# Node pass of a relational graph layer: gathered rows in a pool of their own, two blocks' sums by VectorE, 352 of 2048 weight columns by ScalarE and GpSimd

## The chip, the cores and the metric

One core of a Trainium2 chip runs the whole program in one launch. The time is device microseconds of that core. The engines have queues of their own: PE (TensorE, matmuls and transposes; PEld is its weight load), DVE (VectorE), ACT (ScalarE), POOL (GpSimd) and SP (SyncE, which issues most DMAs). Each works through its instructions in order and waits at semaphores for the others.

## The reference, cut to what matters

A graph layer with relations, a mixture of experts, a second graph network and a ternary feed-forward stage follow each other, each added to x (10000 rows of 512, float32). Only the first is touched:

```python
w = jnp.einsum('rb,bio->rio', att, basis)      # 2 relations, 30 bases of 512 x 512
x_j = x[col]                                   # 5000 edges
for r in range(NUM_RELATIONS):
    gate = jax.nn.sigmoid(x_j @ gate_w[r, :, 0])
    msgs.append(gate[:, None] * x_j @ w[r])
msg = jnp.where((edge_type == 0)[:, None], msgs[0], msgs[1])
agg = jax.ops.segment_sum(msg, row, num_segments=x.shape[0])
return agg + x @ root + bias
...
h = relu(rgcn_gate_layer(x, ..., basis1, att1, gate_w1, root1, bias1))
out = rgcn_gate_layer(h, ..., basis2, att2, gate_w2, root2, bias2)
```

x is layer-normalised before it enters.

## The kernel before

**The node pass** (`rgcn_nodes1`, L775 to L799) goes over 20 blocks of four tiles of 128 rows (the last has two tiles and 16 rows). For each it loads x (tile `x_in`, by `rows_to`, L141), normalises it into `xn` (statistics on DVE, L172 to L178, the scaling on ACT, L183), stores `xn` to `xn_d`, transposes it (PE L198, copies on ACT L202), multiplies by root (PE L790), copies PSUM into `o_nodes` on ACT (L794), adds the bias to the whole block on POOL (L796) and stores to `r1_d`. Loads and stores stand in SP's queue.

**Beside it**, in the same stretch, two sorts of the edges run (`sort_edges`, L224 to L377): one by source with 42 tiles, one by target with 40. Each has a loop of 40 rounds in which PE, ACT and DVE find the place of 128 edges (DVE L353, L358, L362) and POOL scatters their records (L363). Behind the loop POOL loads the sorted table back (L372, tile `srt`). **Also beside it** are the relations' weights (`relation_weights`, L655 to L673): for each of 30 bases a 1 MB load (L663) and on DVE two instructions over 128x2048 (L670), one a relation. Both layers' weights are summed here, but for the last six bases of the second layer, which come in the first edge pass. A scheduler orders all this on every engine, by estimated costs.

**The edge pass** (`rgcn_edges`, L675 to L773) has an order written out by hand for PE, ACT and DVE. For each of 42 tiles it gathers 128 rows (L644, tile `x`, FETCHED = 6 tiles ahead), multiplies them with the gates on DVE (L708), makes the matrix `same` (L719, L721), sums rows of equal target (L728), multiplies by the relation's weights (`put`, L750), copies (L755) and scatter-adds into DRAM (L649). `beside_1` puts other work into the rounds: the six bases, copies of x to `a2_d` (L846) and the placing of nodes. The pass runs twice, on `xn_d` into `r1_d` and, with a relu, on `r1_d` into `a2_d`.

**The next stage** loads root2, bias2 and small weights (L151, L146, L944 on), and then block by block `r_in` from `r1_d` and `x_in` from `a2_d` (L141); ACT takes the relu of `r_in` (L975), PE transposes it and multiplies by root2 (L987).

**Memory.** On-chip memory comes from pools that open and close like a stack. A tile in memory that an earlier pool held waits until that pool's last users are done. `x` and `gate` of the edge pass lie in pools opened after those of the node pass close.

Of the kernel before, what the change touches and what calls it, by code (L numbers as in the profile page):

```python
# [8 lines left out]
F32 = mybir.dt.float32  # L9
# [3 lines left out]
AF = mybir.ActivationFunctionType  # L13
OP = mybir.AluOpType
# [3 lines left out]
P = 128  # L18
N = 10000
D = 512  # L20
KC = D // P
# [14 lines left out]
NB = (N + 511) // 512  # L36
PARTS = 8
PER = NT // PARTS + 1
RELATIONS = 2
# [31 lines left out]
def gnn_ffn_kernel(ctx: ExitStack, tc: tile.TileContext, I, out, dram):  # L71
# [60 lines left out]
            nc.sync.dma_start(d[r0 : r0 + P, :], zero)  # L132


    def rows_to(sb, d, b, store=False):

        for n, a0, a1 in block_parts(b):
            r0 = (b * 4 + a0) * P
            v = d[r0 : r0 + n * (a1 - a0), :].rearrange("(a p) d -> p a d", p=n)
            s = sb[:n, a0:a1, :]  # L140
            nc.sync.dma_start(v, s) if store else nc.sync.dma_start(s, v)  # L141

    def row_broadcast(pool, d, width, name):
# [48 lines left out]
    def transposed(tp, pt, src, tiles, cols, name="xT", on_act=False):  # L192

        xT = tp.tile([P, KC, 512], F32, name=name)
        for k in range(KC):
            ps = pt.tile([P, 512], F32, name="ps_t")
            for a, n in tiles:
                nc.tensor.transpose(  # L198
                    ps[:, a * P : a * P + n], src[:n, a, k * P : (k + 1) * P], ident[:n, :n]
                )  # L200
            if on_act:
                nc.scalar.copy(xT[:, k, :cols], ps[:, :cols])  # L202
            else:
                copy_out(xT[:, k, :cols], ps[:, :cols])
        return xT
# [448 lines left out]

    def relation_weights(basis, att_d, pool, stream, tag):  # L655

        att = row_broadcast(pool, att_d, RELATIONS * BASES, f"att_{tag}")
        ws = pool.tile([P, RELATIONS, KC * D], F32, name=f"w_{tag}")

        def sums():  # L660
            for b in range(BASES):
                t = stream.tile([P, KC, D], F32, name="basis")
                nc.sync.dma_start(t, basis[b].rearrange("(k p) o -> p k o", p=P))  # L663
                tf = t.rearrange("p k o -> p (k o)")
                for r in range(RELATIONS):
                    c = att[:, r * BASES + b : r * BASES + b + 1]
                    if b == 0:
                        nc.vector.tensor_scalar(ws[:, r], tf, c, None, op0=OP.mult)
                    else:
                        nc.vector.scalar_tensor_tensor(ws[:, r], tf, c, ws[:, r], op0=OP.mult, op1=OP.add)  # L670
                yield

        return ws, sums()  # L673

    def rgcn_edges(tag, meta, src_d, relu, ws, gate_d, dst_d, beside):  # L675

# [3 lines left out]
        with ExitStack() as s:  # L680
# [2 lines left out]
            pk = s.enter_context(tc.tile_pool(name=f"re_pk_{tag}", bufs=1, space=PSUM))  # L683
            pa = s.enter_context(tc.tile_pool(name=f"re_pa_{tag}", bufs=2, space=PSUM))
            po = s.enter_context(tc.tile_pool(name=f"re_po_{tag}", bufs=2, space=PSUM))
            gate = row_broadcast(fix, gate_d, RELATIONS * D, "gate")
            of_rel = fix.tile([P, RT, RELATIONS], F32, name="of_rel")
            nc.vector.tensor_scalar(of_rel[:, :, 0], meta["attr"], 0.0, None, op0=OP.is_equal)
            nc.vector.tensor_scalar(of_rel[:, :, 1], meta["attr"], 0.0, None, op0=OP.not_equal)
# [5 lines left out]
            carry_on = {-1: acc}  # L695

            def fetch(t):
                got[t] = wk.tile([P, D], F32, name="x", bufs=FETCHED + 2)
                return gather(got[t], src_d, meta["gidx"][:, t : t + 1])

            def make_ready(t):
# [73 lines left out]
    def rgcn_nodes1(root, bias, pools):  # L775

        ld, tp, small, pt, po = pools
        for b in range(NB):
            tiles, parts, cols = block_tiles(b), block_parts(b), block_cols(b)
            x = ld.tile([P, 4, D], F32, name="x_in")  # L780
            rows_to(x, I["x"], b)
            xn = ld.tile([P, 4, D], F32, name="xn")
            layernorm(small, xn, x, tiles, parts, on_act=True)
            rows_to(xn, xn_d, b, store=True)
            xT = transposed(tp, pt, xn, tiles, cols, on_act=True)
            o = tp.tile([P, 4, D], F32, name="o_nodes")
            for a, n in tiles:
                ps_o = po.tile([P, D], F32, name="ps_o")
                for k in range(KC):
                    nc.tensor.matmul(  # L790
                        ps_o[:n], lhsT=xT[:, k, a * P : a * P + n], rhs=root[:, k, :],
                        start=k == 0, stop=k == KC - 1,
                    )
                nc.scalar.copy(o[:n, a, :], ps_o[:n])  # L794
            for n, a0, a1 in parts:
                nc.gpsimd.tensor_tensor(  # L796
                    o[:n, a0:a1], o[:n, a0:a1], bias[:n, None, :].to_broadcast([n, a1 - a0, D]), OP.add
                )
            rows_to(o, r1_d, b, store=True)  # L799

    with ExitStack() as s:
        wpool = s.enter_context(tc.tile_pool(name="w_rel", bufs=1))
        stream = s.enter_context(tc.tile_pool(name="stream", bufs=3))
        src_meta = s.enter_context(tc.tile_pool(name="src_meta", bufs=1))
        wk = s.enter_context(tc.tile_pool(name="sort", bufs=1))
        place_wk = s.enter_context(tc.tile_pool(name="place_wk", bufs=1))
        ps = s.enter_context(tc.tile_pool(name="sort_ps", bufs=2, space=PSUM))
        with ExitStack() as n:
            ld = n.enter_context(tc.tile_pool(name="ld1", bufs=2))
            tp = n.enter_context(tc.tile_pool(name="tp1", bufs=2))  # L810
            fix = n.enter_context(tc.tile_pool(name="fix1", bufs=1))
            small = n.enter_context(tc.tile_pool(name="small1", bufs=3))
            pt = n.enter_context(tc.tile_pool(name="pt1", bufs=2, space=PSUM))
            po = n.enter_context(tc.tile_pool(name="po1", bufs=3, space=PSUM))
            zero = fix.tile([P, D], F32, name="zero")
            nc.gpsimd.memset(zero, 0.0)
            for d in (r1_d, a2_d, xf_d, x2_d):
                clear_spare(zero, d)
            root = load_square(fix, I["L0_gnn_root1"], "root")
            bias = row_broadcast(fix, I["L0_gnn_bias1"], D, "bias")  # L820
            by_src = sort_edges(
                "s", I["src"], I["dst"], I["edge_type_2"], by_src_d, wk, ps, src_meta, by_relation=True
            )
            by_src = add_targets(by_src, wk, ps, src_meta)
            by_dst = sort_edges(
                "d", I["dst"], I["src"], I["edge_weight1"].rearrange("e o -> (e o)"), by_dst_d, wk, ps,
                meta_pool,
            )
            rgcn_nodes1(root, bias, (ld, tp, small, pt, po))
            ws1, adding = relation_weights(I["L0_gnn_basis1"], I["L0_gnn_att1"], wpool, stream, "1")  # L830
            for _ in adding:
                pass
            ws2, adding = relation_weights(I["L0_gnn_basis2"], I["L0_gnn_att2"], wpool, stream, "2")
            for _ in range(EARLY_BASES):
                next(adding)
        placing = place_nodes(by_dst, place_wk, ps, meta_pool)

        def beside_1(i, ready):
            if i > FETCHED and i % 6 == 2:
                next(adding, None)  # L840
            elif i > FETCHED and i % 2:
                next(placing, None)
            if i < ET:

                c0, c1 = N * i // ET, N * (i + 1) // ET
                cp = nc.sync.dma_start(a2_d[c0:c1, :], I["x"][c0:c1, :])  # L846
                tc.add_manual_dep(
                    cp.ins, ready.ins.name,
                    mybir.DependencyInfo(mybir.DependencyClass.Sync, mybir.DependencyReason.DATA),
                    reason="not all at once, and not beside the nodes",  # L850
                )

        rgcn_edges("1", by_src, xn_d, False, ws1, I["L0_gnn_gate_w1"], r1_d, beside_1)
        for _ in adding:
            pass
        rgcn_edges(
            "2", by_src, r1_d, True, ws2, I["L0_gnn_gate_w2"], a2_d, lambda i, _: next(placing, None)
        )
        for _ in placing:
            pass  # L860
# [1082 lines left out]
```

## Time and profile before

| | us |
|---|---|
| median of 3 runs (4553.06, 4539.74, 4551.91) | 4551.91 |
| profiled execution, and its span | 4526.65, 4524.6 |
| mean granted TensorE clock in it | 0.945 |
| node pass, sorts and weights | 0 to 517 on PE, to 534 on DVE |
| first edge pass | 547 to 785 |
| second edge pass | 786 to 1007 |
| later stages | from 1013 |

The page lists busy time by engine, slices of the span, the chain that ended last, and groups of instructions by line. In a group's row stand the busy time, the mean of one in ns, and after the second bar the idle time of its engine just ahead of it, with what ended it. A line such as `DVE L708 ... [9.58 <-DMA x]` in a timeline says that the engine sat idle for 9.58 us before it until a DMA into x had landed. Two more rows are used in what follows: POOL's other direct DMAs are few (L372 took 2.00 us to issue at 503.2 us), and SP's issues of stores to `r1_d` took 0.50 to 0.70 us each (525.0, 526.2 and 529.6 us). The large loads on SP are the bases (60 of 1 MB each), `x_in` and `r_in` (19 of 1 MB each).

### The profile page before, as it was taken

How to read it: one execution, taken by the hardware profiler on the slowest of the kernel's cores; microseconds unless marked ns; L12 is line 12 of the kernel's file. 1: busy time of each engine (PE TensorE's matmuls, PEld its weight loads, DVE VectorE, ACT ScalarE, POOL GpSimd, SP SyncE). 2: the span in 40 equal slices, each digit the busy share in tenths (PEclk: the TensorE clock that was granted, in tenths of full speed). 3: DMA queues.
4: the chain of work that ended last, by engine and by line, in shares of the span. 5: the costliest groups of instructions: out<-in, count | busy, mean ns of one | idle time of the engine just before them, and what ended most of it. 6: DMA issues, size and time to landing. Idle time of an engine off the chain costs nothing.

```text
span 4524.6 us, 43237 instructions
## 1 busy us (share of the span) xinstructions
PE 4026.9 (89%) x13663; PEld 2048.2 (45%) x13663; DVE 2825.3 (62%) x6089; ACT 1731.2 (38%) x3093; POOL 1558.0 (34%) x1128
## 2 busy tenths in 40 slices
PE   6889698999999927968789999999999999999997
PEld 3443354554444413434444545445554454544443
DVE  9988676755544565647565557545575455755776
ACT  4334222333333311126447223372232722335775
POOL 3424454540000066865551124211242112422443
PEclk9999899998989958989899999999999999999998
DMA  8766685557555316986421233012320123302332
GB/s 283 247 228 207 226 224 126 106 95 241 169 175 178 127 45 124 163 180 214 135 67 49 77 113 85 22 40 77 117 82 21 40 77 115 84 21 58 109 111 96
DMA packets 286241, 560.41 MB, mean 124 GB/s; under 512 B 41776, under 2 KB 72529, under 8 KB 284351
## 3 DMA queue, kind: packets, MB, share of 16 engines
q1 hardware_dynamic: 212304, 367.82, 24.1%
q0 software_dynamic: 73712, 189.84, 18.1%
q8 instruction: 111, 1.82, 0.2%
q14 instruction: 114, 0.93, 0.1%
HBM read 316.03 MB, written 262.00 MB: 128 GB/s over the span
## 4 chain that ended last, share of the span: by engine, by line
PE 38%; DVE 9%; DMA 3%; ACT 2%; issue 2%; POOL 1%; DVEq 0%; POOLq 0%; ACTq 0%
PE ps_b L1409 15%; PE ps_d L1409 9%; PE ps_o L1715 5%; PE ps_e L1409 4%; PE ps_x L1551 2%; PE ps_x L1337 2%; DMA x<-xg_d,gpos 2%; DVE stats L1524 2%; DMA x_in<-x_d,node_at 1%; DVE feat L1341 1%; PE ps_q L1783 1%; DVE feat L1424 1%; ACT feat L1537 1%; DVE x L1326 1%; DVE t L1455 1%
## 5 line engine op out<-in xcount | busy, mean ns | idle before, releaser
L1409 PE MATMUL ps_b<-feat,w 128*128 128x512 f32 (+1 forms) x1120 | 497.6, 586 | 6.9 <-ACT feat L1537 6.9
L1409 PE MATMUL ps_d<-feat,w_s 128*128 128x512 f32 (+1 forms) x1096 | 489.0, 583 | 3.6 <-ACT p L1417 2.7
L1417 ACT ACTIVATE feat<-ps_b,cols 128x512 f32<-128x512 f32 (+1 forms) x300 | 203.9, 681 | 535.3 <-PE ps_b L1409 522.6
L1463 POOL TENSOR_TENSOR feat<-feat 128x1024 f32<-128x1024 f32 (+1 forms) x70 | 162.7, 2324 | 626.5 <-DVE feat L1462 576.6
L790 PE MATMUL ps_o<-root,xT 128*128 128x512 f32 (+1 forms) x632 | 324.8, 630 | 0.0
L1478 POOL TENSOR_TENSOR feat<-feat,p 128x1024 f32<-128x1024 f32 (+1 forms) x66 | 167.2, 2533 | 455.4 <-ACT feat L1417 455.3
L1409 PEld LDWEIGHTS ps_b<-feat,w 128*128 128x128 f32 x1120 | 209.6, 192 | 239.2 <-issue 208.7
L750 PE MATMUL ps_o<-w,aT 128*128 x672 | 311.0, 607 | 1.1 <-issue 0.9
L670 DVE SCALAR_TENSOR_TENSOR w<-basis,att,w 128x2048 f32<-128x2048 f32 x116 | 307.0, 2657 | 0.0
L1553 DVE TENSOR_TENSOR x_rows<-ps_x,be 128x512 f32<-128x512 f32 (+1 forms) x237 | 157.6, 686 | 234.6 <-PE ps_x L1551 229.4
L1409 PE MATMUL ps_b<-t,w_s 128*128 128x512 f32 (+1 forms) x560 | 257.3, 600 | 33.5 <-ACT feat L1417 33.5
L1409 PEld LDWEIGHTS ps_d<-feat,w_s 128*128 128x128 f32 x1096 | 198.4, 191 | 195.2 <-issue 171.5
L987 PE MATMUL ps_n<-root,rT 128*128 128x512 f32 (+1 forms) x632 | 285.1, 607 | 0.0
L644 POOL DMA_INDIRECT x<-xg_d,gpos x160 | 177.6, 1110 | 259.4 <-PE ps_x L1337 49.6
L1409 PE MATMUL ps_e<-feat,w 128*128 128x512 f32 (+1 forms) x560 | 255.4, 595 | 9.2 <-DVE feat L1372 9.2
L1409 PE MATMUL ps_b<-feat,w_s 128*128 128x512 f32 (+1 forms) x560 | 250.0, 586 | 0.0
L1537 ACT ACTIVATE feat<-feat,bn_sm 128x512 f32<-128x512 f32 (+2 forms) x320 | 237.6, 805 | 3.6 <-DVE bn_sm L1515 3.6
L1524 DVE BATCH_NORM_STATS2 stats<-feat 128x6 f32<-128x512 f32 (+1 forms) x320 | 203.7, 668 | 41.5 <-POOL feat L1478 28.3
L1337 PEld LDWEIGHTS ps_x<-same,x 128*128 128x128 f32 x1280 | 164.3, 196 | 104.9 <-ACT x L1332 55.2
L1337 PE MATMUL ps_x<-same,x 128*128 128x128 f32 x1280 | 171.4, 283 | 42.9 <-ACT x L1332 36.8
L172 DVE BATCH_NORM_STATS2 ln_st<-x_in 128x6 f32<-128x512 f32 (+1 forms) x237 | 160.2, 683 | 69.1 <-DMA x_in<-x_d,node_at 58.0
L1332 ACT ACTIVATE x<-x 128x512 f32<-128x512 f32 x160 | 99.0, 628 | 244.1 <-DVE x L1326 178.7
(514 smaller groups left out, 7710.6 us busy)
## 6 DMA issues: line engine op xcount, KB each, us to landing
basis<-in_L_gnn_basis SPq DMA_DIRECT2D x60, 1024.0 KB
xg_d<-x_rows SPq DMA_DIRECT2D x234, 256.0 KB
a_d<-in_x SPq DMA_DIRECT2D x40, 500.0 KB
xg_d<-x_in SPq DMA_DIRECT2D x39, 512.0 KB
x_in<-in_x SPq DMA_DIRECT2D x19, 1024.0 KB
xn_d<-xn SPq DMA_DIRECT2D x19, 1024.0 KB
r_d<-o_nodes SPq DMA_DIRECT2D x19, 1024.0 KB
r_in<-r_d SPq DMA_DIRECT2D x19, 1024.0 KB
```

What stands on the lines that cost most here:

```text
L644: return nc.gpsimd.indirect_dma_start(out=dst, out_offset=None, in_=src, in_offset=bass.IndirectOffsetOnAxis(ap=idx, axis=0))
L670: nc.vector.scalar_tensor_tensor(ws[:, r], tf, c, ws[:, r], op0=OP.mult, op1=OP.add)
L750: nc.tensor.matmul(ps_o, lhsT=aT[:, k, :], rhs=w_all[:, bass.ds(w0 + k * D, D)], start=k == 0, stop=k == KC - 1,)
L790: nc.tensor.matmul(ps_o[:n], lhsT=xT[:, k, a * P : a * P + n], rhs=root[:, k, :], start=k == 0, stop=k == KC - 1,)
L987: nc.tensor.matmul(ps_o[:n_], lhsT=rT[:, k, a * P : a * P + n_], rhs=root[:, k, :], start=k == 0, stop=k == KC - 1,)
L1337: nc.tensor.matmul(ps_a[:, k, :], lhsT=x[:, k * P : (k + 1) * P], rhs=same, start=True, stop=True)
L1409: nc.tensor.matmul(ps[fo], lhsT=A[a][:, k, fo * P : (fo + 1) * P], rhs=x[:, k, :], start=first and k == 0, stop=k == 1, skip_group_check=True,
L1417: nc.scalar.activation(dst[:, fo, :], ps[fo], func, bias=b, scale=scale)
L1478: (nc.vector if last else nc.gpsimd).tensor_tensor(b22, b22, p5, OP.add)
L1524: nc.vector.bn_stats(stats[:, k, 2 * p + j, :], big[:, k, s0 + j * w : s0 + (j + 1) * w])
L1537: nc.scalar.activation(hb, hb, AF.Relu, bias=sm[:, fo, 3:4], scale=sm[:, fo, 2:3])
L1715: nc.tensor.matmul(ps_o[:n_], lhsT=big[:, kc, t * P : t * P + n_], rhs=W2[kc], start=kc == 0, stop=kc == KC - 1,)
```

## The change

Three things are changed in the first layer.

1. A pool `rows` is opened outside the node pass. It holds `gate` and the gathered tiles `x`, FETCHED + 1 = 7 of them instead of 8. The gate of the first layer is loaded at the start, that of the second between the passes. To make room, the node pass normalises in place (`x_in` instead of `xn`, two buffers of each before, two in all after) and the tile of zeros is taken from `x_in`'s pool.
2. For the last two blocks, 18 and 19, the seven sums with the bias go from PSUM to `o_nodes` on DVE, in place of ACT's copies and POOL's additions, and their three stores to `r1_d` are issued by POOL.
3. Of 2048 columns of the relations' weights DVE keeps 1696. ACT scales the other 352 into a tile `part` (one buffer, both relations), POOL adds it for both relations at once (2 x 352 columns). For the first basis ACT writes into the weights and POOL adds nothing.

```diff
-    def rows_to(sb, d, b, store=False):
+    def rows_to(sb, d, b, store=False, queue=nc.sync):
...
-            nc.sync.dma_start(v, s) if store else nc.sync.dma_start(s, v)
+            queue.dma_start(v, s) if store else queue.dma_start(s, v)
...
         ws = pool.tile([P, RELATIONS, KC * D], F32, name=f"w_{tag}")
+        split = KC * D - 352
...
                 tf = t.rearrange("p k o -> p (k o)")
+                part = stream.tile([P, RELATIONS, KC * D - split], F32, name="part", bufs=1)
                 for r in range(RELATIONS):
                     c = att[:, r * BASES + b : r * BASES + b + 1]
+                    w, wp = ws[:, r, :split], ws[:, r, split:]
+                    nc.scalar.activation(
+                        wp if b == 0 else part[:, r], tf[:, split:], AF.Identity, bias=0.0, scale=c
+                    )
                     if b == 0:
-                        nc.vector.tensor_scalar(ws[:, r], tf, c, None, op0=OP.mult)
+                        nc.vector.tensor_scalar(w, tf[:, :split], c, None, op0=OP.mult)
                     else:
-                        nc.vector.scalar_tensor_tensor(ws[:, r], tf, c, ws[:, r], op0=OP.mult, op1=OP.add)
+                        nc.vector.scalar_tensor_tensor(w, tf[:, :split], c, w, op0=OP.mult, op1=OP.add)
+                if b:
+                    nc.gpsimd.tensor_tensor(ws[:, :, split:], ws[:, :, split:], part, OP.add)
                 yield
...
-            gate = row_broadcast(fix, gate_d, RELATIONS * D, "gate")
...
-                got[t] = wk.tile([P, D], F32, name="x", bufs=FETCHED + 2)
+                got[t] = rows.tile([P, D], F32, name="x", bufs=FETCHED + 1)
...
             rows_to(x, I["x"], b)
-            xn = ld.tile([P, 4, D], F32, name="xn")
-            layernorm(small, xn, x, tiles, parts, on_act=True)
-            rows_to(xn, xn_d, b, store=True)
-            xT = transposed(tp, pt, xn, tiles, cols, on_act=True)
+            layernorm(small, x, x, tiles, parts, on_act=True)
+            rows_to(x, xn_d, b, store=True)
+            xT = transposed(tp, pt, x, tiles, cols, on_act=True)
...
-                nc.scalar.copy(o[:n, a, :], ps_o[:n])
-            for n, a0, a1 in parts:
+                if b < NB - 2:
+                    nc.scalar.copy(o[:n, a, :], ps_o[:n])
+                else:
+                    nc.vector.tensor_tensor(o[:n, a, :], ps_o[:n], bias[:n], OP.add)
+            for n, a0, a1 in parts if b < NB - 2 else ():
                 nc.gpsimd.tensor_tensor(
                     o[:n, a0:a1], o[:n, a0:a1], bias[:n, None, :].to_broadcast([n, a1 - a0, D]), OP.add
                 )
-            rows_to(o, r1_d, b, store=True)
+
+            rows_to(o, r1_d, b, store=True, queue=nc.gpsimd if b >= NB - 2 else nc.sync)
...
+        rows = s.enter_context(tc.tile_pool(name="rows", bufs=1))
         with ExitStack() as n:
...
-            zero = fix.tile([P, D], F32, name="zero")
+            zero = ld.tile([P, 4, D], F32, name="x_in")[:, 0, :]
...
+            gate = row_broadcast(rows, I["L0_gnn_gate_w1"], RELATIONS * D, "gate")
             rgcn_nodes1(root, bias, (ld, tp, small, pt, po))
...
-        rgcn_edges("1", by_src, xn_d, False, ws1, I["L0_gnn_gate_w1"], r1_d, beside_1)
+        rgcn_edges("1", by_src, xn_d, False, ws1, gate, r1_d, rows, beside_1)
         for _ in adding:
             pass
+        gate = row_broadcast(rows, I["L0_gnn_gate_w2"], RELATIONS * D, "gate")
         rgcn_edges(
-            "2", by_src, r1_d, True, ws2, I["L0_gnn_gate_w2"], a2_d, lambda i, _: next(placing, None)
+            "2", by_src, r1_d, True, ws2, gate, a2_d, rows, lambda i, _: next(placing, None)
         )
```

Line numbers of the profile of the changed kernel are 7 to 14 higher in this part.

More of the change, by code (lines that the diff above doesn't have):

```diff
@@ L664, in sums, with rgcn_edges @@
                 tf = t.rearrange("p k o -> p (k o)")
+                part = stream.tile([P, RELATIONS, KC * D - split], F32, name="part", bufs=1)
                 for r in range(RELATIONS):
                     c = att[:, r * BASES + b : r * BASES + b + 1]
+                    w, wp = ws[:, r, :split], ws[:, r, split:]
+                    nc.scalar.activation(
+                        wp if b == 0 else part[:, r], tf[:, split:], AF.Identity, bias=0.0, scale=c
+                    )
                     if b == 0:
-                        nc.vector.tensor_scalar(ws[:, r], tf, c, None, op0=OP.mult)
+                        nc.vector.tensor_scalar(w, tf[:, :split], c, None, op0=OP.mult)
                     else:
-                        nc.vector.scalar_tensor_tensor(ws[:, r], tf, c, ws[:, r], op0=OP.mult, op1=OP.add)
+                        nc.vector.scalar_tensor_tensor(w, tf[:, :split], c, w, op0=OP.mult, op1=OP.add)
+                if b:
+                    nc.gpsimd.tensor_tensor(ws[:, :, split:], ws[:, :, split:], part, OP.add)
                 yield
         return ws, sums()
-    def rgcn_edges(tag, meta, src_d, relu, ws, gate_d, dst_d, beside):
+    def rgcn_edges(tag, meta, src_d, relu, ws, gate, dst_d, rows, beside):
         with ExitStack() as s:
```

## The prediction

> **What bounds the kernel now.** I read the page's sums first, then the slices, then windows over the only part that the change touches, and last the timeline of the place where that part ends.
>
> ```profile
> PE 4026.9 (89%) x13663; PEld 2048.2 (45%) x13663; DVE 2825.3 (62%) x6089; ACT 1731.2 (38%) x3093; POOL 1558.0 (34%) x1128
> ...
> PE   6889698999999927968789999999999999999997
> ...
> DVE  9988676755544565647565557545575455755776
> ```
>
> The whole is bound by PE, but the first four or five slices (to 517 us) are not: there DVE is as full as PE. The windows (us, then busy PE, PEld, DVE, ACT, POOL, then granted clock, DMA share, GB/s) say it stage by stage:
>
> ```profile
> 0.00:100.00 100.00, 69.12 (x279) 39.96 (x280) 92.71 (x209) 39.50 (x85) 26.32 (x25) 1.00 0.90 294
> 100.00:200.00 100.00, 87.54 (x304) 45.69 (x303) 94.83 (x194) 42.63 (x98) 46.93 (x30) 0.93 0.73 243
> ...
> 400.00:500.00 100.00, 95.34 (x299) 38.84 (x298) 89.30 (x153) 38.48 (x87) 48.51 (x27) 0.98 0.55 182
> 500.00:550.00 50.00, 19.44 (x58) 8.95 (x57) 25.66 (x28) 6.07 (x13) 20.25 (x12) 0.69 0.73 241
> ```
>
> DVE is at 95% around the end of the first sort and PE stands nearly still from 517 to 547. The timelines of PE, DVE and POOL there:
>
> ```profile
> 547.28 0.47 PE L719 MATMUL ps_k<-ident,key_s 128*128 128x128 f32 x1 [30.35 <-DVE same L721]
> ```
> ```profile
> 512.35 21.27 DVE L670 SCALAR_TENSOR_TENSOR w<-basis,att,w 128x2048 f32<-128x2048 f32 x8
> ...
> 543.50 0.69 DVE L708 SCALAR_TENSOR_TENSOR prod<-x,gate 128x512 f32<-128x512 f32 x1 [9.58 <-DMA x<-xn_d,gidx_s]
> ```
> ```profile
> 539.94 1.02 POOL L644 DMA_INDIRECT x<-xn_d,gidx_s  x1 [19.78 <-DMA r_d<-o_nodes]
> ```
>
> So two things hold back the first edge pass: eight sums that DVE still owes (to 533.6), and a gather that waits 19.8 us for the last store of node sums, because its tile lies in memory of the node pass. The gathers' wait alone costs 9.6 us: without it DVE would go on at 533.8.
>
> **What DVE pays beside GpSimd.** Grouped by form over 0 to 547 us:
>
> ```profile
> L670 DVE SCALAR_TENSOR_TENSOR w<-basis,att,w 128x2048 f32<-128x2048 f32 x104 | 279.4, 2694 | 0.0
> L796 POOL TENSOR_TENSOR o_nodes<-o_nodes,bias 128x2048 f32<-128x2048 f32 x19 | 100.1, 5267 | 138.6 <-ACT o_nodes L794 117.8 <-issue 20.5
> L362 DVE TENSOR_TENSOR pos_i<-pos,before 128x1 int32<-128x1 f32 x80 | 32.3, 404 | 0.0
> ```
>
> A lone L670 takes 2.34 us, a lone L362 0.15, a lone 128x2048 L796 4.5. The excess of the first two is 279.4 - 104 x 2.34 = 36 and 32.3 - 80 x 0.15 = 20 us; two rarer lines (L265, L419) add 8. The timeline shows where it goes, each taking the other's time whole:
>
> ```profile
> 152.38 6.94 DVE L670 SCALAR_TENSOR_TENSOR w<-basis,att,w 128x2048 f32<-128x2048 f32 x1
> ...
> 152.63 4.53 POOL L796 TENSOR_TENSOR o_nodes<-o_nodes,bias 128x2048 f32<-128x2048 f32 x1
> ```
>
> 6.94 is 2.35 + 4.53. DVE instructions that read PSUM, and the layernorm's statistics, show no such stretch. In all DVE loses 65 us to some 91 us of lone bias adds: 0.7 us per us.
>
> **The change part by part.** Times are from the profiled execution, span 4524.6 us in 4526.65; that lies 25 us under the median of the runs shown (4551.91), so I form a difference and add it to the median.
>
> *The relations' weights.* DVE's sum shrinks from 2048 to 1696 columns: 2.34 x 1696/2048 = 1.94, so -0.40 on each of 104 before the edges, -42 us. ScalarE gets two 128x352 scalings per basis: between its copies of 272 columns (0.39) and 512 (0.59), about 0.5, 52 us in a stage where it is 39% busy: covered. GpSimd gets one addition of 2 x 352 = 704 columns per basis: 704 x 4.53/2048 = 1.56 us, 52 of them (81 us) before the edges, 6 in the first edge pass. What each takes from DVE no row shows at this length: at least 0 (it falls under instructions that read PSUM or into DVE's 64 us of idle), at most its whole 1.56. By the 0.7 above it is 1.1. A 4.5 us addition cannot miss a sum, a short one can: reads of PSUM, statistics and idle time are some 37% of DVE's time, which leaves 1.0, and its first part may still run under a scan of another kind: I take 0.9, 47 us. The break-even is 0.8 a basis, what the two shorter sums save.
>
> The Trainium skill (SBUF — State Buffer, section "SBUF: two separate sides") speaks against this part: GpSimd and a DVE instruction with two SBUF inputs share a port pair by an exclusive lock held for the whole instruction. The 6.94 us row agrees. Read strictly, each of the 52 would cost DVE its full 1.56 us, and the sum below would end some 34 us later.
>
> *The order that the scheduler gives.* Between the ends of the two sorts the changed program's order on each engine differs, so I count by stretch. To the end of the first sort's loop (before 53.5 to 254 us) 39 sums stand where 32 stood, 20 statistics where 28, with 20 additions: +7 x 1.94 - 32 x 0.40 - 8 x 0.67 + 20 x 0.9 = +13, and one bias add more (3): +16. From there to the second sort's loop 17 for 20, 16 for 22, 8 additions and one bias add fewer: -7 - 7 - 4 + 7 - 3, about -14 to -18. In the second loop (to 488) 37 for 35, 24 for 16 and 20 additions: +4 - 14 + 5 + 18 = +13, of which the loop's idle time (DVE waits 30.8 us in all at L353 for PE) may take a few. The last L362 moves from 488 to about 498: **+10**.
>
> *Behind the last L362.* Before, DVE's first edge work is 55.5 us behind it. After, five sums, the end of block 18 and block 19 are left. Sort rows land about 18 us behind (before 24); the sums (5 x 1.94), their additions and block 18's seven to eight small instructions end at +28, ScalarE's four L183 (0.81 each) at +32; only then does SP, in order, store block 18's rows and load block 19's. That load is late because x_in has two buffers and no xn: it lands near +38, statistics and normalising take to +45, transposes and 12 matmuls (0.43 each) to +57, the last of the seven DVE adds from PSUM (0.69 each, L991's kind is the nearest) to +58.5. The gathers, with rows in memory of their own, wait only for the last xn_d stores (+49) and land at +53, hidden. So the 9.6 us wait goes, and the last block's chain takes its place: **+3**. If the load is not late this is -5; if ScalarE waits for GpSimd's additions in between it is +15.
>
> *Stores on GpSimd's queue.* Three stores at the price of POOL's one plain DMA there (L372, 2.00 us) are 6 us between the seventh gather and the eighth, against 0.5 to 0.7 on SP. Seven tiles are then in hand, 5.6 us each (235/42): no cost; without that cover 6 us. The first scatter waits for them as it did. The Trainium skill (DMA: Bandwidth & Descriptors, "Rules for kernel authors") gives such spreading no bandwidth, only issue time on the queue left; here SP's queue bears no wait that this would free, which the 0.5 us issues agree with.
>
> *PE's clock.* Granted 0.69 in 500 to 550; the first eight L750 behind the gap take 6.66 us, warm ones 3.60. With the gap split up: **-4** (0 to -6).
>
> *First edge pass.* Six bases: 2 x -0.40 and up to +1.56 each, two ScalarE scalings between its copies: -5 to +5, I take **+1**. Seven x buffers for eight bind nothing, as the buffer's last reader stands one round earlier.
>
> *The next stage's head.* Before, root2 (1 MB) is issued at 502.98 and the small weights up to 720; r_in is issued at 1013.53 and ScalarE waits for it:
>
> ```profile
> 1019.42 1.91 ACT L975 ACTIVATE r_in<-r_in 128x2048 f32<-128x2048 f32 x1 [11.46 <-DMA r_in<-r_d]
> ```
>
> After, root2 and six small loads take memory that the edge passes hold; they wait for the last scatter, as r_in does, and stand ahead of it on SP: seven issues at 0.4 to 0.6 are 3.5 us, and 1.4 MB of transfer at the window's 274 GB/s 5 us, part beside the issues. **+6** (3 to 9). Nothing hides it: PE has no other work there.
>
> Sum: 10 + 3 - 4 + 1 + 6 = **+16**, 4568 us.
>
> **The rivals.** A measurement of this kernel can tell about 0.3%, 13.7 us, from no change.
>
> *DVE is relieved* (faster, 0.32). If a 704-column addition costs DVE 0.3 us, the last L362 comes at +10 - 48 x 0.6 = -19, block 19's load is less late (-2), clock -5, edge pass -2, head +6: -22, 4530 us. For it: the additions stand in GpSimd's queue between scatters that wait for L362, so many can start while DVE waits for PE (30.8 us). Against: the 0.7 measured. It decides below 0.45 us.
>
> *A balance* (no change, 0.18). At 0.6 us: -4 + 3 - 4 - 1 + 6 = 0, 4552 us. For it: break-even is near the price.
>
> *The exclusion in full* (slower still, 0.08). At 1.56 us: +10 + 32 + 3 - 4 + 4 + 6 = +51, of which idle time may take 6: 4597 us. Against it: bias adds do not cost their full time either.
>
> *That the additions hold up the sort's scatters* is no rival of its own: no instruction of the loop waits for an L363, only L372 at its end does, which an addition of 1.56 us ahead of it delays by that much once in each sort.
>
> **How the numbers follow.** The forecast has 0.42, its own range 4556 to 4588. Slower is 0.42 + 0.08 = 0.50, within 0.3% 0.18, faster 0.32. The range goes from 4522 to 4590: it leaves out the far end of the first rival, the third, and little else, about 0.2.
>
> **What would show it.** L677 at 1.94 us alone and above 2.2 in the mean; GpSimd's new line at 1.6 to 2.1 us; the last L362 near 498; first gathers issued before the last node sums; PE's 30 us gap split; seven loads ahead of r_in and PE's first transposes of that stage 6 us later behind the last put. Wrong if L677 stays below 2.1 in the mean, if the first edge pass starts before 540, or if r_in lands as early as before.

## The result, and the profile after

The changed kernel took 4623.4 us (median of four runs, 4623.1 to 4624.6) where the kernel before took 4550.3 beside it: ratio 1.0165, 95% interval 1.0151 to 1.0178, some 73 us slower. The forecast was 4568, slower by 16. The direction held, the size did not.

The profiled execution has a span of 4622.8 us, 98 more than the one before. By stage, from the first instruction of one to the first of the next:

| | before | after | difference | forecast |
|---|---|---|---|---|
| last L362 of the second sort | 488.0 | 531.2 | +43.2 | +10 |
| from there to DVE's first edge work (L708, now L716) | 55.5 | 78.3 | +22.8 | +3 |
| first edge pass (to the first L719, now L727, of the second) | 242.9 | 252.0 | +9.1 | +1, and -4 for the clock |
| second edge pass (first to last L719/L727) | 205.0 | 205.6 | +0.6 | 0 |
| from there to the first weight load of L987, now L1001 | 32.5 | 39.5 | +7.0 | +6 |
| the rest, whose work is the same | 3500.7 | 3516.2 | +15.5 | 0 |

The rest is no effect that these traces can tie to the change: it is longest (3516 and 3511 us) in this run and in half_the_columns below, the two on whose chip before took 4550 and 4545 us, and lies between 3485 and 3506 in all other profiles. So it seems to go with the chip. The stages above it make 83 us, the medians say 73.

The first edge work comes 66 us later (609.5 against 543.5 us). Of these, DVE is busy for 41 more (511.2 us up to there against 470.3) and idle for 25 more (98.3 against 73.2). The two parts have different causes; the experiments show the first, and the second only in part.

The lines that answer to those shown of before, first the windows (us, then busy PE, PEld, DVE, ACT, POOL, granted clock, DMA share, GB/s):

```profile
0.00:100.00 100.00, 57.84 (x212) 31.79 (x212) 85.61 (x164) 37.98 (x77) 43.53 (x27) 0.92 0.69 230
100.00:200.00 100.00, 79.08 (x271) 42.21 (x272) 97.16 (x169) 49.44 (x113) 68.33 (x38) 0.89 0.71 225
...
400.00:500.00 100.00, 88.59 (x270) 33.96 (x269) 91.39 (x168) 49.53 (x112) 79.09 (x37) 0.96 0.65 219
500.00:550.00 50.00, 34.24 (x96) 14.45 (x96) 36.78 (x56) 15.68 (x33) 27.41 (x15) 0.81 0.51 163
```

DVE is as full as before (97 of 100 us in the second row) with smaller sums, and PE has fallen from 87.5 to 79.1 in that row: part of DVE's busy time is not work. The groups by form over 0 to 620 us show what it is:

```profile
L677 DVE SCALAR_TENSOR_TENSOR w<-basis,att,w 128x1696 f32<-128x1696 f32 x104 | 272.7, 2624 | 0.0
L679 POOL TENSOR_TENSOR w<-w,part 128x704 f32<-128x704 f32 x52 | 122.6, 2358 | 99.4 <-ACT part L671 94.4 <-ACT hiT L349 3.7 <-issue 0.6
L671 ACT ACTIVATE part<-basis,att 128x352 f32<-128x352 f32 x104 | 58.7, 585 | 60.0 <-POOL w L679 55.4 <-DMA basis<-in_L_gnn_basis 4.6
L362 DVE TENSOR_TENSOR pos_i<-pos,before 128x1 int32<-128x1 f32 x80 | 44.6, 558 | 0.1
L178 DVE SCALAR_TENSOR_TENSOR ln_mv<-ln_mv,ln_rs 128x4 f32<-128x4 f32 x19 | 24.4, 1282 | 0.0
```

A sum over 1696 columns takes 1.97 us where nothing disturbs it, close to the 1.94 worked out; its mean is 2.62, hardly better than the 2.69 of 2048 columns. L362 should take 0.14 us and L178 0.15. The excess of the three is 272.7 - 104 x 1.973 = 68, 44.6 - 80 x 0.14 = 33 and 24.4 - 19 x 0.15 = 21: 122 us. In the kernel before the same count gives 57 us (36, 21 and 0; L178 took 0.155 us there in the mean). An addition alone takes 1.68 us (the estimate was 1.56), its mean is 2.36. The timeline shows one beside one sum:

```profile
65.96 3.47 DVE L677 SCALAR_TENSOR_TENSOR w<-basis,att,w 128x1696 f32<-128x1696 f32 x1
65.97 1.67 POOL L679 TENSOR_TENSOR w<-w,part 128x704 f32<-128x704 f32 x1
```

Behind the sort, the timeline of PE:

```profile
550.32 1.11 PE L198 MATMUL ps_t<-ident,x_in 128*128 128x128 f32 x4 [15.14 <-ACT xT L202]
...
576.41 13.04 PE L797 MATMUL ps_o<-root,xT 128*128 128x512 f32 x30
...
592.27 9.81 PE L797 MATMUL ps_o<-root,xT 128*128 128x512 f32 x22
602.02 0.32 PE L727 MATMUL ps_k<-ident,key_s 128*128 128x128 f32 x1
613.44 0.48 PE L727 MATMUL ps_k<-ident,key_s 128*128 128x128 f32 x1 [11.10 <-DVE same L729]
```

of DVE:

```profile
545.31 0.20 DVE L374 COPY key_d<-srt_d 128x40 f32<-128x40 f32 x1 [8.93 <-DMA srt_d<-by_dst_d]
...
567.72 1.29 DVE L172 BATCH_NORM_STATS2 ln_st<-x_in 128x6 f32<-128x512 f32 x2 [10.65 <-DMA x_in<-in_x]
...
609.52 0.69 DVE L716 SCALAR_TENSOR_TENSOR prod<-x,gate 128x512 f32<-128x512 f32 x1 [6.71 <-DMA r_d<-o_nodes]
```

and of POOL, whose first gather this is:

```profile
585.55 1.01 POOL L644 DMA_INDIRECT x<-xn_d,gidx_s  x1 [6.87 <-DMA xn_d<-x_in]
```

PE's idle stretch of 30 us is down to 11, and the gathers run 24 us ahead of need. But another 15 us of idle stand earlier, at 550, and PE works on nodes until 602 instead of 517, and the wait for the last stores of node sums has not gone: it moved from the gathers to DVE's first `prod`. At the head of the next stage, in ACT's timeline:

```profile
1101.31 1.91 ACT L989 ACTIVATE r_in<-r_in 128x2048 f32<-128x2048 f32 x1 [17.65 <-DMA r_in<-r_d]
```

### The profile page after: what moved, and what is told of

The parts are those of the page before. It is cut to its first block, busy times and chain, and to the rows that moved or that the text cites. A ratio compares the mean times of both kernels' runs of the same rounds, so it can differ in the third digit from the quotient of the medians.

```text
span 4622.8 us, 43545 instructions
## 1 busy us (share of the span) xinstructions
PE 4057.6 (88%) x13663; PEld 2059.4 (45%) x13663; DVE 2871.1 (62%) x6096; ACT 1786.5 (39%) x3207; POOL 1700.1 (37%) x1186
## 4 chain that ended last, share of the span: by engine, by line
PE 57%; DVE 13%; DMA 7%; issue 4%; ACT 3%; POOL 2%; another core or an unknown queue 1%; SPq 0%; ACTq 0%; DVEq 0%; POOLq 0%
PE ps_b L1423 15%; PE ps_d L1423 9%; PE ps_o L758 5%; PE ps_o L1729 5%; PE ps_e L1423 4%; PE ps_n L1001 3%; PE ps_x L1565 2%; DMA x_d<-x_in 2%; PE ps_x L1351 2%; PE ps_o L1037 2%; PE ps_h L1302 2%; DVE stats L1538 2%; DMA x<-xg_d,gpos 1%; PE ps_a L736 1%; PE ps_y L1312 1%
## 5 line engine op out<-in xcount | busy, mean ns | idle before, releaser
L797 PE MATMUL ps_o<-root,xT 128*128 128x512 f32 (+1 forms) x632 | 339.9, 655 | 11.3 <-ACT xT L202 8.3
L758 PE MATMUL ps_o<-w,aT 128*128 x672 | 313.8, 611 | 1.3 <-issue 1.1
L677 DVE SCALAR_TENSOR_TENSOR w<-basis,att,w 128x1696 f32<-128x1696 f32 x116 | 296.0, 2557 | 0.8 <-DMA basis<-in_L_gnn_basis 0.8
L1001 PE MATMUL ps_n<-root,rT 128*128 128x512 f32 (+1 forms) x632 | 286.2, 609 | 0.0
```

Source lines behind the costliest of these rows:

```text
L677: nc.vector.scalar_tensor_tensor(w, tf[:, :split], c, w, op0=OP.mult, op1=OP.add)
L758: nc.tensor.matmul(ps_o, lhsT=aT[:, k, :], rhs=w_all[:, bass.ds(w0 + k * D, D)], start=k == 0, stop=k == KC - 1,)
L797: nc.tensor.matmul(ps_o[:n], lhsT=xT[:, k, a * P : a * P + n], rhs=root[:, k, :], start=k == 0, stop=k == KC - 1,)
L1001: nc.tensor.matmul(ps_o[:n_], lhsT=rT[:, k, a * P : a * P + n_], rhs=root[:, k, :], start=k == 0, stop=k == KC - 1,)
```

## The experiments

Before's time differs from chip to chip (4522 to 4550 us), so each kernel is given by its ratio to the runs of before on the same chip.

### Which part costs the time

**no_columns** takes part 3 out of the changed kernel, **columns_alone** puts part 3 alone into the kernel before.

```diff
-        split = KC * D - 352
...
-                part = stream.tile([P, RELATIONS, KC * D - split], F32, name="part", bufs=1)
...
-                if b:
-                    nc.gpsimd.tensor_tensor(ws[:, :, split:], ws[:, :, split:], part, OP.add)
```

> The changed kernel with part 3 undone: DVE sums all 2048 columns again, no scaling on ScalarE, no addition on GpSimd; the pool for the gathered rows, the in-place normalising and the last two blocks' sums and stores stay. Exclusion theory (each 704-column addition costs DVE about 1.5 us): the last L362 falls back from 531 to about 488 us, the loss of the tail and of the next stage's head stays: 4560 to 4580 us. Rival (the columns cost little, the loss comes from two x_in buffers and the new order): still above 4600 us.

> The kernel before with part 3 alone. Exclusion theory: last L362 near 530 us, six additions in the first edge pass cost some 5 us more, no loss at the head of the next stage: 4590 to 4605 us. Rival (the loss comes from two x_in buffers and the new order): 4550 to 4560 us.

no_columns: 1.0016 (1.0000 to 1.0033). Some 7 us of loss are left, less than the 10 to 30 that the expectation gave to parts 1 and 2; the excess of the three lines is back to 59 us. columns_alone: 1.0119 (1.0091 to 1.0147), some 54 us, a time that the theory allowed and far from the rival. So the loss comes with the columns. But columns_alone does not lose it in the way that the theory said: the last L362 comes at 489, as before, and the first edge work (here L716) at 579.0, 35.5 us later than before. Its groups by form up to there:

```profile
L676 DVE SCALAR_TENSOR_TENSOR w<-basis,att,w 128x1696 f32<-128x1696 f32 x104 | 245.2, 2366 | 0.0
L362 DVE TENSOR_TENSOR pos_i<-pos,before 128x1 int32<-128x1 f32 x80 | 63.1, 789 | 0.1
...
L178 DVE SCALAR_TENSOR_TENSOR ln_mv<-ln_mv,ln_rs 128x4 f32<-128x4 f32 x19 | 7.3, 386 | 0.0
```

The excess is 40 + 52 + 4 = 96 us, 39 over the 57 of before: 0.76 us an addition, about what the shorter sums save. DVE is busy for only 9 us more than before (479.0 against 470.3); the other 27 of the 35.5 are idle time of DVE behind the last L362, where PE still owes 120 of the 632 matmul rows of the nodes, against 56 before (the last ends at 571 instead of 517). So the columns cost in two ways: in DVE's own instructions, and by an order in which more node work is left for the end. How much falls to each differs from kernel to kernel, and the last L362 is a poor marker between kernels of different order.

In the next stage's head the first weight load of that stage comes 31.9 us behind the second pass's last transpose in no_columns, 40.3 in columns_alone. So the late root2 comes with the tile `part` and not with the pool `rows`.

### Reading, or waiting

**memset_for_add** keeps every wait between ACT and POOL and takes away what POOL reads; the 352 columns are left unsummed.

```diff
-                    nc.gpsimd.tensor_tensor(ws[:, :, split:], ws[:, :, split:], part, OP.add)
+                    nc.gpsimd.memset(part, 0.0)
```

> The changed kernel, in which GpSimd fills the tile part with zeros instead of adding it to the weights (the 352 columns of the weights are left wrong). GpSimd still waits for ScalarE's scaling, ScalarE still waits for GpSimd, but GpSimd reads nothing. Exclusion theory: L677 and L362 lose their excess (69 and 33 us of it fall to about a half, what the bias adds cost), the last L362 comes near 480 us, time 4555 to 4580 us. Rival (the chain ScalarE to GpSimd and back over one buffer holds the stage up): ScalarE still waits tens of us for GpSimd and the time stays above 4600 us.

1.0014 (1.0002 to 1.0027): the loss is gone. Its groups by form, same window:

```profile
L677 DVE SCALAR_TENSOR_TENSOR w<-basis,att,w 128x1696 f32<-128x1696 f32 x108 | 244.3, 2265 | 0.0
L671 ACT ACTIVATE part<-basis,att 128x352 f32<-128x352 f32 x108 | 60.9, 585 | 31.6 <-POOL part L679 24.0 <-DMA basis<-in_L_gnn_basis 7.4
L679 POOL MEMSET part<- 128x704 f32 x54 | 37.3, 690 | 107.3 <-ACT part L671 105.9 <-ACT o_nodes L802 1.3
L362 DVE TENSOR_TENSOR pos_i<-pos,before 128x1 int32<-128x1 f32 x80 | 28.9, 361 | 0.1
L178 DVE SCALAR_TENSOR_TENSOR ln_mv<-ln_mv,ln_rs 128x4 f32<-128x4 f32 x19 | 10.4, 547 | 0.0
```

The excess of the three lines is 31 + 18 + 8 = 57 us, and 122 - 57 = 65 us over 52 additions is **1.25 us an addition**. The 57 are what the 18 bias adds leave (the 21 of before cost as much). ACT still waits 24 us for POOL, and that costs nothing that shows. The last L362 comes at 474.6 us, 56.6 earlier than with the additions: most of the 65 us lies on the chain.

A memset is also shorter than an addition (0.69 us against 1.68), so it could harm less for that reason alone. The trace speaks against it: the 34 sums that run beside a memset and no bias add take 1.95 to 1.98 us, as long as those beside nothing.

```profile
163.68 1.97 DVE L677 SCALAR_TENSOR_TENSOR w<-basis,att,w 128x1696 f32<-128x1696 f32 x1
163.86 0.70 POOL L679 MEMSET part<- 128x704 f32 x1
```

In the changed kernel the 44 sums beside an addition and no bias add take 2.60 us in the mean.

One more thing is read here. With the additions' harm taken away DVE is busy for 31 us less than before (439.4 us up to its first edge work), and the time is still not under before: the last L362 gains 13.4 us, and the 78.4 us from there to DVE's first edge work, as long as in the changed kernel, take them back.

The first edge pass shows the price on other instructions. Its L716 in the changed kernel, groups by form over the pass:

```profile
L716 DVE SCALAR_TENSOR_TENSOR prod<-x,gate 128x512 f32<-128x512 f32 x84 | 65.4, 779 | 8.2 <-DMA r_d<-o_nodes 6.7
```

and in memset_for_add:

```profile
L716 DVE SCALAR_TENSOR_TENSOR prod<-x,gate 128x512 f32<-128x512 f32 x84 | 57.7, 687 | 8.6 <-DMA r_d<-o_nodes 7.2
```

That is 7.7 us for six additions, and the short L722 lost another 2.0 (8.8 us against 6.8): 1.6 each, almost an addition's whole length. The pass as a whole is 15.6 us shorter with the memsets (236.4 us against 252.0).

**half_the_columns** gives away 176 columns in as many additions (`split = KC * D - 176`).

> The changed kernel with 176 of 2048 columns given away, and as many additions (52 before the edges) of half the width. Theory (DVE loses about three quarters of every addition's lone time, at any width): an addition takes 0.8 to 0.95 us alone and costs DVE 0.6 to 0.75; the excess of DVE's instructions before the edges falls by 25 to 35 us against the changed kernel; DVE saves 0.4 a basis instead of 0.8, so the loss is about half of that of the columns: 0.9% to 1.3% over before. Rival (a fixed loss each time the engines hand the memory over, at any width): the excess stays within 12 us of the changed kernel's and the time is 1.6% to 2.0% over before.

1.0100 (1.0063 to 1.0137). An addition takes 0.94 us alone. Its groups by form, 0 to 620 us:

```profile
L677 DVE SCALAR_TENSOR_TENSOR w<-basis,att,w 128x1872 f32<-128x1872 f32 x106 | 275.2, 2603 | 0.0
...
L362 DVE TENSOR_TENSOR pos_i<-pos,before 128x1 int32<-128x1 f32 x80 | 41.1, 514 | 0.0
L178 DVE SCALAR_TENSOR_TENSOR ln_mv<-ln_mv,ln_rs 128x4 f32<-128x4 f32 x19 | 14.8, 778 | 0.0
```

A sum of this width takes 2.154 us undisturbed, so the excess is 47 + 30 + 12 = 89 us, 33 under the changed kernel's; over memset_for_add's 57 that is 32 us for 53 additions, 0.6 each. So in these kernels the price goes with the length: 1.25 of 1.68 us, 0.6 of 0.94, and 65 of 91 for the bias adds of before, two thirds to three quarters of POOL's lone time. In the order of columns_alone it was less, 0.76 of 1.69. DVE saves 0.7 us a basis at 352 columns (2 x (2.34 - 1.97)) and 0.4 at 176, under the price both times in the order of the changed kernel; two widths do not prove it for every one.

### The bias adds, from which the price was taken

**bias_on_dve** is the kernel before with every block's bias added by DVE from PSUM.

```diff
-                nc.scalar.copy(o[:n, a, :], ps_o[:n])
-            for n, a0, a1 in parts:
-                nc.gpsimd.tensor_tensor(
-                    o[:n, a0:a1], o[:n, a0:a1], bias[:n, None, :].to_broadcast([n, a1 - a0, D]), OP.add
-                )
+                nc.vector.tensor_tensor(o[:n, a, :], ps_o[:n], bias[:n], OP.add)
```

> The kernel before with every node block's bias added by DVE from PSUM (79 instructions of about 0.69 us, 54 us) in place of ScalarE's copies and GpSimd's additions. Exclusion theory (the bias adds take 65 us from DVE): L670 and L362 fall to their lone 2.34 and 0.15 us, DVE's busy time before the edges falls by some 10 us, the last L362 comes 5 to 15 us earlier and the time is 0.1% to 0.35% under before. Rival (the excess of L670 and L362 has another cause, or covers waits): the excess stays, DVE has 54 us more to do, time 0.6% to 1.2% over before.

0.9936 (0.9922 to 0.9949), more than expected. The groups by form (0 to 500 us) show the excess gone (2.33 and 0.15 us are the lone times):

```profile
L670 DVE SCALAR_TENSOR_TENSOR w<-basis,att,w 128x2048 f32<-128x2048 f32 x92 | 213.9, 2334 | 0.0
L362 DVE TENSOR_TENSOR pos_i<-pos,before 128x1 int32<-128x1 f32 x80 | 11.7, 146 | 0.0
```

DVE does 54 us more of adds, and still its busy time up to the first edge work is 428.8 us instead of 470.3. Twelve sums (28 us) of the difference have moved into the first edge pass; the other 13 us are a true saving: POOL's additions cost DVE more than the work that they take off. The last L362 comes at 425.6 instead of 488.0, but 24 sums fewer stand ahead of it, so it says nothing about the price. ACT is free of 79 copies here too, and no run separates that from DVE's relief.

### The tail behind the sort

**stores_alone** issues the last two blocks' stores of before from POOL; **late_read_back** also reads the second sort's table back only behind the weights.

```diff
-            rows_to(o, r1_d, b, store=True)
+            rows_to(o, r1_d, b, store=True, queue=nc.gpsimd if b >= NB - 2 else nc.sync)
...
+        by_dst = by_dst()
         placing = place_nodes(by_dst, place_wk, ps, meta_pool)
```

> The kernel before with one thing changed: the stores of the node sums of blocks 18 and 19 are issued by GpSimd, right behind its bias adds, and not by SP behind loads of bases. Theory (the gathers of the first edge pass wait for these stores, which SP issues 8 to 15 us late): stores issued at 511 to 521 us, first gather near 530, first L708 at about 534 instead of 543.5, time 4538 to 4543 us. Rival (the gathers' wait only covers what DVE owes, and GpSimd's issues delay the bias adds): no change, 4547 to 4553 us.

> The kernel before with the stores of blocks 18 and 19 on GpSimd's queue and, in addition, the reading back of the second sort's table (L372 to L376) put behind the relations' weights in the program. Theory (DVE's idle 12.9 us for srt_d, with eight sums behind it, and then the gathers' wait set the start of the first edge pass): DVE runs its eleven sums without a stop and the first L708 comes 15 to 20 us earlier behind the last L362 than before (55.5 us), time 0.3% to 0.45% under before. Rival (the gap is refunded later, since the edge passes wait for the copies and GpSimd anyway): within 0.1% of before.

stores_alone: 0.9995 (0.9982 to 1.0009), no change that can be told. The first gather comes at 532.5 instead of 539.9 and DVE no longer waits for it, as the theory says. But the last L362 itself comes 7 us later, so the first L708 gains 3 us (540.4 against 543.5) and not the 9 expected. late_read_back: 0.9973 (0.9962 to 0.9985), a little less than what was expected, and the profile does not show where: the first edge work (here L711) comes at 544.0, as before, 47.1 us behind a last L362 that is 9 us later. DVE's eleven sums, now in one run, take 36.6 us beside POOL's bias adds instead of 32.4 in two runs, and the first gather is late again (536.2).

**in_place_alone** normalises in place in the kernel before (`layernorm(small, x, x, ...)`, no `xn`).

> The kernel before with the node pass normalised in place, so that two buffers of x_in serve where two of x_in and two of xn did; nothing else. Theory (a load must now wait for the transposes and the store of two blocks ago, so the scheduler leaves more blocks behind the sort): PE ends the node pass 20 to 30 us later than at 516, and since the gathers still wait for the last stores the time is 0.4% to 0.7% over before. Rival (it is the last blocks' sums on DVE that stretch the tail): PE ends at 513 to 523, time within 0.15% of before.

0.9982 (0.9971 to 0.9993): a miss. PE ends the node pass 18 us later, close to what was expected, but the first edge work comes only 3 us later than before (546.9 against 543.5), and the time does not rise. Two buffers are no loss. That the time falls lies, in the profile, in the later stages, whose work is the same (3485 us against 3501), and can't be put down to the change.

**prod_in_rows** gives `prod` memory of its own in the changed kernel.

```diff
-                got[t] = rows.tile([P, D], F32, name="x", bufs=FETCHED + 1)
+                got[t] = rows.tile([P, D], F32, name="x", bufs=FETCHED)
...
-                prod = wk.tile([P, D], F32, name="prod", bufs=2)
+                prod = rows.tile([P, D], F32, name="prod", bufs=1)
```

> The changed kernel with prod (one buffer) in the pool rows too, and six buffers of x to make room. Theory (the first L716 waits 6.7 us for the last stores of node sums, since prod lies in memory of the node pass): DVE's wait ahead of the first L716 falls from 6.7 to under 2 us, first L716 some 72 us behind the last L362 instead of 78, time 3 to 7 us under the changed kernel (ratio to before 0.1% lower). Rival (the wait is for the gathers on the same semaphores, not for prod's memory): still 6 to 7 us.

DVE's first L716 comes at 590.2 us, 58.6 behind the last L362 and not 78.3, between two node sums and with no wait. So the wait was for prod's memory. The second pass starts 4 us earlier; the ratio, 1.0156 (1.0133 to 1.0179), cannot be told from the changed kernel's.

**head_on_act_queue** issues the loads of root2 and the small weights at the next stage's head from ACT's queue.

> The changed kernel, in which root2, bias2 and the five small loads at the head of the next stage are issued by ScalarE's queue and not by SP's. Theory (seven issues stand ahead of r_in): r_in is issued right behind the last scatter's landing and the first L1001 comes 33 to 36 us behind the last transpose of the second pass instead of 38.8, time 3 to 6 us under the changed kernel. Rival (the 1.4 MB of transfer, not the issues, hold r_in up): still 38 to 39 us, no change.

r_in is issued 22.0 us behind the second pass's last transpose instead of 26.0, but the first weight load comes after 37.2 us instead of 39.5 (the 38.8 of the expectation is a semaphore's row just ahead of it), and the ratio is 1.0167 (1.0151 to 1.0183). The rival has most of it: the issues hold up 2 us. The remaining 5 over before are most likely the 1 MB of root2 that must arrive beside r_in, but no run took that transfer away alone.

### A version that beats both

With POOL out of the way, DVE still owes sums when PE is done with the nodes. Three runs put bias_on_dve and late_read_back together; two of them also take bases out of the part ahead of the first edge pass and give them to its rounds.

```diff
-EARLY_BASES = 24
+EARLY_BASES = 16
...
-            if i > FETCHED and i % 6 == 2:
+            if i > FETCHED and i % 3 == 2:
```

> Every bias add on DVE from PSUM, with the late reading back and the last stores on GpSimd's queue besides. Theory (the two gains lie on different waits and add): DVE does not stop for srt_d (11.2 us in the bias run), the first L708 comes near 488 us instead of 499, time 0.8% to 1.0% under before. Rival (behind the earlier start the first edge pass waits for weights that DVE still owes): no better than the bias run, 0.55% to 0.7% under before.

> The same with ten of the second layer's bases summed in the first edge pass in place of six (one in four rounds). Theory (DVE is at 67% in the edge pass and bound before it): a further 0.1% to 0.4%, 1.0% to 1.3% under before. Rival (the sums delay prod and same in the hand-written order of the pass): the pass grows by as much as the start moves, no gain over the run beside it.

> The same with fourteen bases in the first edge pass (one in three rounds). Theory: another 0.1% if DVE has room in the pass (14 x 4.7 = 66 us beside 157 us of 235). Rival: worse than ten, as the pass becomes bound by DVE.

0.9924 (0.9902 to 0.9947), 0.9919 (0.9897 to 0.9942) with `EARLY_BASES = 20` and one round in four, and 0.9895 (0.9871 to 0.9919) with fourteen bases: about 48 us under before. The first step is within the interval of bias_on_dve; ten bases add nothing that can be told from it; fourteen give the lowest time (4472 to 4481 us in four runs, with ten 4481 to 4488 on the same chip).

The traces show why ten did nothing: they did not move a sum. In bias_and_read_back 26 sums (13 bases, not six) already run inside the first edge pass, because the scheduler had let the sums that DVE still owed run into it; 16 of them stand together in its first 60 us. With ten bases it is 26 again, with fourteen 28, now spread over the rounds. From the first edge work to the last transpose of the second pass it takes 477, 473 and 462 us in the three. Whether the even spread or the placing of nodes, which thereby moves towards the second pass, brought the last step was not separated.

## Why the prediction was wrong in size

**Which stage bounds, and that DVE and POOL exclude each other: right.** The forecast's 1.94 us for the smaller sum was nearly met (1.97). ScalarE's scalings (0.585 us each) were not run alone; memset_for_add, which has them all, is level with before.

**The price of an addition: this is the step that failed.** The trace of before gave 0.7 us lost per us of POOL, so 1.1. The prediction then set this aside for an argument: a short addition meets an instruction that can be held up only 63% of the time, which makes 1.0 of 1.56, and 0.9 with its first part taken off. No row showed that additions fall in that proportion. The runs show 1.25 in the changed kernel, where 0.9 stood in the sum: 1.25 of 1.68 is 0.74, close to the 0.7 of the old bias adds, and the lone time too was 0.12 longer than worked out. Part of the harm fell on an instruction that the prediction did not count: L178, 21 us, where the trace of before shows none. The page on which the exclusion rests (the Trainium skill, SBUF — State Buffer, "SBUF: two separate sides") says that it holds only against GpSimd work that reads SBUF; the memset agrees, and its strict reading, 1.56 us each, was a little nearer than 0.9 for the changed kernel. For columns_alone, with 0.76, it was not.

**The order.** At 45 us of chain for each us of price (56.6 / 1.25) the slope of 48 was good, so the error of 0.35 us explains 16 of the 33 us by which the last L362 was missed. The other half is the offset: with the additions' harm gone the last L362 stands at -13, where the same count of sums and statistics gives +10 - 48 x 0.9 = -33. About half of that offset is waiting: up to its last L362 DVE waits at L353 for PE for 39.8 us in memset_for_add, 30.6 before, a wait that the prediction thought might shrink. The rest was not isolated.

**The tail: wrong, by omissions.** It is the second step that failed, +22.8 for +3. Block 19's load, statistics and normalising came within 2 us of what was worked out (landed 36.5 us behind the last L362, against 38). But PE still owed the matmuls of blocks 17 and 18, and only block 19's twelve were counted, at 0.43 us each; the trace has 24 rows for them (2 and 22), two for each: nodes end at +71, not +57. PE came to them late because DVE, in order, stopped 8.9 us for the sorted table with block 18's statistics behind that stop; ACT's copies waited for those and PE for the copies, 15.1 us. And the prediction followed the gathers to their new memory without asking what else lies in the old: `prod` does, and inherits the wait (6.7 us). Five profiles with the columns, and with prod where it was, have 69 to 90 us from the last L362 to the first edge work; before, no_columns, stores_alone, late_read_back and in_place_alone have 44 to 56, and the four with every bias add on DVE, which have 19 to 23 sums left there, 55 to 73. With the columns 93 to 120 of PE's node rows are left behind the last L362, in the other five 44 to 66. Why the scheduler leaves more blocks behind with the columns is not settled, and with it stays open why columns_alone loses most of its time.

**The first edge pass: +9.1 for +1.** Without the additions' reads the pass would be 6.5 us shorter than before (memset_for_add), with them it is 9.1 longer: 15.6 us for the six, where the forecast allowed at most 1.56 each. L716 and L722 show 9.7 of it as their own. Of the clock's 4 us little came: the first eight L758 take 5.14 us where 6.66 stood, 1.5 us.

**The next stage's head: right in size** (7.0 for 6), with a different split: 2 us of issues, the rest probably transfer. It comes with `part`; the pool `rows` alone, in no_columns, does not cause it.

**Stores on GpSimd's queue, two x_in buffers: no cost**, as argued for the first; the second was feared and is none. The seven x buffers were not run alone; no_columns has all three at 1.0016.

**The rivals.** The case in which the exclusion is paid in full (4597 us, chance 0.08) came nearest, and was underrated; but that is partly luck, for its price of 1.56 was not reached before the edges (1.25), and the tail, which it left at +3, made up for it. The case of relief is refuted from its root: memset_for_add has the relief and does not win.

## What to carry to other kernels

Before work is moved to GpSimd beside a busy VectorE, compare what VectorE saves with GpSimd's whole time for it, less what the trace shows to slip through, and take a measured ratio as it is. Here moving 352 columns over saved 0.7 us a basis and cost 1.25, and about 0.8 in another order; moving the old bias adds back from GpSimd onto VectorE, reading PSUM, was worth 0.6%. Where a scheduler orders the engines, compare also what it leaves behind the last wait: that cost columns_alone more than the exclusion did. And when a tile gets memory of its own to lose a wait, look for the next tile in the old memory: it inherits the wait.

## What the runs showed of the hardware that was not expected

A VectorE instruction of one element per partition (L362, 0.14 us) is held up like a long one: it lost 33 us over 80 instructions. The exclusion also works the other way, on POOL's indirect DMAs: in bias_on_dve the scatters L363 that run beside a sum stand in GpSimd's timeline for 2.65 us in the mean, the others for 0.99, and the first gather for 15.7 us, the later ones for about 0.95:

```profile
480.58 15.71 POOL L644 DMA_INDIRECT x<-xn_d,gidx_s  x1 [44.67 <-DMA r_d<-o_nodes]
496.59 0.96 POOL L644 DMA_INDIRECT x<-xn_d,gidx_s  x1 [0.30 <-issue]
```

beside nine sums in a row in VectorE's:

```profile
474.97 20.43 DVE L670 SCALAR_TENSOR_TENSOR w<-basis,att,w 128x2048 f32<-128x2048 f32 x9
```

The gather is through 1 us after the last sum. In the three runs of the version that beats both it is the same, with 10.9, 11.1 and 5.8 us. So a run of sums on VectorE just ahead of an edge pass delays the gathers that the pass waits for.
